# Moving the last layer's closing product of the last three images behind everything else, by channel chunk

## The chip, the core and the metric

The kernel runs on one core of a Trainium2 chip. A core has engines that run side by side, each in its own instruction order: TensorE (PE in the profile: matmuls; PEld: its weight loads), VectorE (DVE), ScalarE (ACT), GpSimd (POOL) and SyncE (SP), which here issues nearly all transfers; 16 DMA engines carry these between DRAM, where inputs and outputs live, and the on-chip memory (SBUF). Matmul results land in PSUM, a small memory of banks, and have to be evacuated by DVE or ACT. Engines wait for each other by semaphores. The metric is the device time of one execution in microseconds (us); a difference of about 0.2% can be told from none.

## What is computed

Two layers on eight images of 512 channels and 32 x 32 = 1024 positions, all in fp32. The first is an attention block, the second a non-local block with a batch normalization at its end. Cut to what matters:

```python
# layer 0
q, k, v = conv1x1(x, Wq, bq), conv1x1(x, Wk, bk), conv1x1(x, Wv, bv)   # 8 heads of 64
attn = softmax(einsum('bhdn,bhdm->bhnm', q, k) * 64 ** -0.5)
x = x + conv1x1(einsum('bhnm,bhdm->bhdn', attn, v), Wp, bp)
# layer 1
g, theta, phi = conv1x1(x, g_w, g_b), conv1x1(x, theta_w, theta_b), conv1x1(x, phi_w, phi_b)
f = einsum('bcn,bdn->bcd', theta, phi) / 1024          # 256 x 256 per image
z = conv1x1(einsum('bcd,bdn->bcn', f, g), W_w, W_b) + x
mean, var = z.mean(axis=(0, 2, 3)), z.var(axis=(0, 2, 3))
out = (z - mean) * rsqrt(var + 1e-5) * gamma + beta
```

The mean and the variance of a channel are over all eight images. No output value is known before the z of the last image is, and all 16.78 MB of output (eight images of four chunks of 128 channels, 512 KB each) are written after it.

## The kernel before, in words

The program is one stream written out for the images 0 to 7. A planner places the instructions of each engine, with semaphores for what depends on what; matmuls are kept in the order in which they are written (`pe`). On-chip memory is handed out by pools: a pool with n buffers makes the allocation number n + 1 wait until the first is free. The ones that matter here:

- `ring` (11 blocks of 512 KB, `block`): the exponentials `e`, and after the attention the sums `t_o`, `t_x`, the weight `ww` and the product `wf`.
- `w3` (tag `acc`, 3): the running sums `acc` of the exponentials, and later in the image the two halves of `g`.
- `wr` (tag `w`, 2): the weights in use, which are fetched from DRAM again for every image (`load_w`).
- `xp` (2): the x of the image at work and of the next one. `mats` has one buffer each for `v`, `q`, `k` and `o`; the tile `tp` takes the place of `o`.
- `psS`: three PSUM tiles of two banks, taken in turn (`next_bank`), for scores and large products; `psO`: two more.

For every image: attention (scores, L300; exp on ACT, L303; weighted sums, L332 to L335), with the q and v products of the next image drawn in near its end; the k product of the next image; `project` (L399), which adds the projection to x in place; `theta_phi`; then `nonlocal_` (L424): g (`pg`), f (`pf`, L434), wf = f times W (`pwf`, L452), and z = wf times g + x (`pz`).

Large products are made by `seven` (L169): seven products of half-size blocks in the place of eight, the blocks being sums that DVE makes beforehand (`data_sums`, L151; for the z product L466 and L469). Each product is evacuated or added up by DVE or ACT.

For images 0 to 6 the z product is one of these (L486): 14 matmuls, evacuated into x, whose statistics (`bn_stats`, L489) follow. z of images 0 to 5 is then written to DRAM (`spill`, L491); z of image 6 stays in its buffer (`KEEP = 2`). For image 7 `last_z` makes the plain product, 16 matmuls, chunk by chunk; as soon as a chunk has its statistics, `batch_norm` (L508) turns mean and variance into scale and shift, applies them to the eight tiles of that chunk, DVE and ACT taking turns, and writes each tile out (L523). Before this, from the end of image 7's attention on, z of images 0 to 5 is fetched back: three into `v`, `q` and `k`, one into `fold`, image 5 into four ring blocks (L537), image 3 into the place of `o`, once `pf` has used up `tp`.

All those transfers are on SP's queue, and SP issues them in the planned order: one that waits holds up those behind it.

A matmul in fp32 makes two entries in the trace, so the profile's counts of matmuls are twice those of the program.

Of the kernel before, what the change touches and what calls it, by code (L numbers as in the profile page):

```python
# [8 lines left out]
F32 = mybir.dt.float32  # L9
I32 = mybir.dt.int32  # L10
AF = mybir.ActivationFunctionType
# [5 lines left out]
P = 128  # L17
# [13 lines left out]
def unshifted(ctx: ExitStack, tc: tile.TileContext, a: dict, out: bass.AP):  # L31
# [8 lines left out]
    NPAIR = HEADS // 2  # L40
    CI = a["WgT"].shape[1]
    IC = CI // P
    KEEP = 2
    RUN = 6
    LEAD = 128

# [17 lines left out]
    def pe(ins):  # L64
        tc.keep_in_program_order(ins)
# [6 lines left out]
    def next_bank(name):  # L72
        free.append(free.pop(0))
        return bank(free[-1], name)

    def block(name):
        return ring.tile([P, 2, 512], F32, tag="e", name=name)
# [153 lines left out]
        nc.vector.memset(heads[j * D:(j + 1) * D, j * D:(j + 1) * D], 1.0)  # L231
    mv = const.tile([P, CC, 2], F32, tag="mv", name="mv")
    gates = const.tile([P, B * NPAIR], F32, tag="gates", name="gates")
    spill = [dram.tile([P, CC, N], F32, tag=f"spill{b}", name=f"spill{b}") for b in range(B - KEEP)]

    def halves(t):
        return t.rearrange("p (h n) -> p h n", h=NH)
# [183 lines left out]
              lambda q, ps: nc.vector.tensor_tensor(at(q), at(q), as_tp(ps), ALU.add))  # L421
        return tp

    def nonlocal_(b, xt, data, tp, wg, before_z):  # L424
        ww = block(f"ww_{b}")
        nc.sync.dma_start(ww, a["WwT"].rearrange("(c p) f -> p c f", p=P))
        g = [w3.tile([P, N], F32, tag="acc", name=f"g_{b}_{d}") for d in range(IC)]
        f = w2.tile([P, IC, CI], F32, tag="ri", name=f"f_{b}")

        def make_f():  # L430
            ps = psO.tile([P, 512], F32, tag="o", name=f"pf_{b}").rearrange("p (c d) -> p c d", c=IC)
            for c in range(IC):
                for i in range(NB):
                    pe(nc.tensor.matmul(ps[:, c, :], tp[:, i, c * P:(c + 1) * P], tp[:, i, CI:],  # L434
                                        start=(i == 0), stop=(i == NB - 1)))
            nc.scalar.mul(f, ps, 1.0 / N)

        def part(q):
            return g[int(q[0]) - 1][:, cols(q)]

        def first(q, ps):
            d = int(q[0]) - 1
            nc.scalar.activation(part(q), ps[:, 0, :], AF.Identity, bias=gb[:, d:d + 1])  # L443

        seven(f"pg_{b}", wg, data, False, first,
              lambda q, ps: nc.vector.tensor_tensor(part(q), part(q), ps[:, 0, :], ALU.add), {5: make_f})

        wf = block(f"wf_{b}")
        for d in range(IC):
            ps = psO.tile([P, 512], F32, tag="o", name=f"pwf_{b}_{d}")  # L450
            for c in range(IC):
                pe(nc.tensor.matmul(ps, f[:, c, d * P:(d + 1) * P], ww[:, c, :], start=(c == 0), stop=(c == IC - 1)))  # L452
            nc.scalar.copy(wf[:, d, :], ps)
        if before_z:
            before_z()
            last_z(b, xt, wf, g)
            return
        half = C // 2
        ws = block(f"ws_{b}")
        w = [wf[:, 0, :half], wf[:, 1, :half], wf[:, 1, half:]] + [ws[:, i, j * half:(j + 1) * half]  # L460
                                                                 for i in range(2) for j in range(2)]
        tg = block(f"tg0_{b}"), block(f"tg1_{b}")
        t = [tg[i // 2][:, i % 2, :] for i in range(4)]
        b11, b12, b21, b22 = (g[k][:, h * 512:(h + 1) * 512] for k in range(2) for h in range(NH))
        for to, l, r in ((t[0], b12, b11), (t[1], b22, t[0]), (t[2], b22, b12), (t[3], b21, t[1])):
            nc.vector.tensor_tensor(to, l, r, ALU.subtract)  # L466
        for to, l, r, op in ((3, wf[:, 0, half:], w[2], ALU.add), (4, w[3], w[0], ALU.subtract),
                             (5, w[0], wf[:, 0, half:], ALU.subtract), (6, w[1], w[4], ALU.subtract)):
            nc.vector.tensor_tensor(w[to], l, r, op)  # L469

        class Blocks:
            shape = (P, 7, 1, half)

            def __getitem__(self, at):
                _, i, k, m = at
                return w[i][:, m]

        def first_z(q, ps):
            for m in range(2):
                c = rows(q).start + m  # L480
                at = xt[:, c, cols(q)]
                nc.vector.scalar_tensor_tensor(at, ps[:, m, :], wb[:, c:c + 1], at, ALU.add, ALU.add)  # L482

        data = {"11": b11, "21": b21, "22": b22, "t1": t[0], "t2": t[1], "t3": t[2], "t4": t[3]}
        data = {n: d.rearrange("p (k n) -> p k n", k=1) for n, d in data.items()}
        seven(f"pz_{b}", Blocks(), data, False, first_z, add_to(xt))  # L486
        for oc in range(CC):
            for h in range(NH):
                nc.vector.bn_stats(stats[:, oc, b * NH + h, :], xt[:, oc, h * 512:(h + 1) * 512])  # L489
            if b < B - KEEP:  # L490
                nc.sync.dma_start(spill[b][:, oc, :], xt[:, oc, :])  # L491

    def last_z(b, xt, wf, g):

        z[b] = [xt[:, oc, :] for oc in range(CC)]
        for oc in range(CC):
            for h in range(NH):
                ps = next_bank(f"pz_{b}_{oc}_{h}")[:, 0, :]
                s = slice(h * 512, (h + 1) * 512)
                for d in range(IC):  # L500
                    pe(nc.tensor.matmul(ps, wf[:, d, oc * P:(oc + 1) * P], g[d][:, s],
                                        start=(d == 0), stop=(d == IC - 1)))
                nc.vector.scalar_tensor_tensor(xt[:, oc, s], ps, wb[:, oc:oc + 1], xt[:, oc, s],
                                               ALU.add, ALU.add)
                nc.vector.bn_stats(stats[:, oc, b * NH + h, :], xt[:, oc, s])
            batch_norm(oc)

    def batch_norm(oc):  # L508

        nc.vector.bn_aggr(mv[:, oc, :], stats[:, oc, :, :].rearrange("p s k -> p (s k)"))  # L510
        gs, shift = (small.tile([P, 1], F32, tag=n, name=f"{n}_{oc}") for n in ("gs", "shift"))
        nc.scalar.activation(gs, mv[:, oc, 1:2], AF.Sqrt, bias=eps)
        nc.vector.reciprocal(gs, gs)
        nc.vector.tensor_tensor(gs, gs, gamma[:, oc:oc + 1], ALU.mult)
        nc.vector.tensor_tensor(shift, mv[:, oc, 0:1], gs, ALU.mult)
        nc.vector.tensor_tensor(shift, beta[:, oc:oc + 1], shift, ALU.subtract)
        for i, b in enumerate(sorted(z, reverse=True)):
            t = z[b][oc]
            if i % 2:
                nc.scalar.activation(t, t, AF.Identity, bias=shift, scale=gs)  # L520
            else:
                nc.vector.tensor_scalar(t, t, gs, shift, ALU.mult, ALU.add)
            nc.sync.dma_start(out_v[b, :, oc, :], t)  # L523

    z = {}

    def reload(b, tag):
        t = mats.tile([P, CC, N], F32, tag=tag, name=f"z_{b}")
        for cc in range(CC):
            nc.sync.dma_start(t[:, cc, :], spill[b][:, cc, :])  # L530
        z[b] = [t[:, cc, :] for cc in range(CC)]
# [5 lines left out]
            nc.sync.dma_start(t, spill[b][:, cc, :])  # L537
            z[b].append(t)

    def reload_fold(b):  # L540
        t = foldp.tile([P, CC, N], F32, tag="fold", name=f"z_{b}")
        for cc in range(CC):
            nc.sync.dma_start(t[:, cc, :], spill[b][:, cc, :])
        z[b] = [t[:, cc, :] for cc in range(CC)]


    data = data_sums(quarters_of(xt), "x_0")
    q, peak_q = heads_of(0, "q", weights("WqT"), bq, data, order=(0, 5, 1, 2, 3, 4, 6))
    load_w(nc.sync)
    bv, bp, gb, wb, gamma, beta = (load_col(n, nc.sync) for n in ("bvc", "bp", "gb", "Wb", "gamma", "beta"))  # L550
    tpb = const.tile([P, 2, 1, CI], F32, tag="tpb", name="tpb")
    nc.sync.dma_start(tpb[:, 0, 0, :], a["theta_b"].partition_broadcast(P))
    nc.sync.dma_start(tpb[:, 1, 0, :], a["phi_b"].partition_broadcast(P))
# [4 lines left out]
    for b in range(B):  # L558
# [19 lines left out]
        if not last:  # L578
            v = nxt["v"]
            k, peak_k = heads_of(b + 1, "k", weights("WkT"), bk, nxt["data"])  # L580
            load_w(nc.sync)
            q, peak_q = nxt["q"], nxt["peak_q"]
            between = {4: lambda: bound_scores(b + 1, q, k, peak_q, peak_k)}
        else:
            for i, tag in enumerate("vqk"):
                reload(i, tag)
            reload_fold(4)
            reload_chunks(5)
        w = weights("WpT")
        if b == 0:  # L590
            join_bias(w)
        project(b, xt, o, w, between)
        load_w(nc.sync)
        data = data_sums(quarters_of(xt), f"x1_{b}")
        tp = theta_phi(b, weights("tp"), data)
        load_w(nc.sync)
        nonlocal_(b, xt, data, tp, weights("WgT"), (lambda: reload(3, "o")) if last else None)
        load_w(nc.sync)
        if B - KEEP <= b < B - 1:
            z[b] = [xt[:, cc, :] for cc in range(CC)]  # L600
        xt = nxt.get("x")


    good = const.tile([P, 1], F32, tag="good", name="good")
# [216 lines left out]
```

## Time and profile before

The time before is 2242.79 us, the median of three runs (2241.12 to 2243.93). The profiled execution has a span of 2242.5 us.

| what | before |
|---|---|
| PE busy, entries | 2187.0 us (98%), 8306 |
| DVE busy, instructions | 1306.7 us (58%), 1273 |
| ACT busy, instructions | 692.8 us (31%), 814 |
| DMA, moved in all | 202.26 MB, mean 90 GB/s |
| mean clock granted to PE | 0.989 |
| z of image 7 begins | 2186.3 us |
| first output issued | 2196.9 us |
| last output issued in the stretch that begins | 2228.1 us |

The views used below are: the page, with the busy time of each engine and the chain of work that ended last, followed back from the last instruction; the same chain in order of time, one line for each piece (start, length, engine, tile and line); the timeline (all instructions in order of time, merged where alike); and stretches, the busy time of each engine between two times, with the clock granted to PE, the share of the DMA engines that is busy and what they moved. The groups list instructions by line, engine, operation and tile with the count, then the busy time in us and the mean of one in ns, then the idle time before them. Names of tiles stand as output<-inputs.

### The profile page before, as it was taken

The page shows a single profiled execution, that of the slowest core. Times are in us where ns is not written, and L with a number is a line of the kernel's source. Part 1 is how long each engine was busy: PE and PEld are TensorE (multiplying, and loading weights), DVE is VectorE, ACT ScalarE, POOL GpSimd, SP SyncE. Part 2 cuts the span into 40 slices and gives each one's busy share as a digit, 9 for nine tenths or more (in the row PEclk, how much of TensorE's full clock was granted, in tenths as well). Part 3 has the DMA queues.
Part 4 walks back from the last instruction along what each step waited for, and adds up shares of the span by engine and source line. Part 5 has one row for each costly group of instructions (what it writes and reads, how often), then busy time and mean ns, then how long its engine had stood idle before and what let it go on. Part 6 is the DMA issues. An engine that isn't in the chain of part 4 may idle for free.

```text
span 2242.5 us, 21033 instructions
## 1 busy us (share of the span) xinstructions
PE 2187.0 (98%) x8306; PEld 1108.8 (49%) x8306; DVE 1306.7 (58%) x1273; ACT 692.8 (31%) x814; POOL 35.4 (2%) x36
## 2 busy tenths in 40 slices
PE   8999999999999999999999999999999999999992
PEld 3634664346633556335563365533664346643361
DVE  4476446763477644775447744577356664467734
ACT  1453104531045210552106510254103531035303
POOL 0000000000000000000000000000000000000000
PEclk9999999999999999999999999999999999999996
DMA  6212223122131222322223221322214122210517
GB/s 234 85 29 89 92 99 127 36 78 89 59 133 46 77 73 91 104 62 66 83 79 108 58 88 64 120 59 62 90 59 150 29 61 90 91 52 20 211 51 313
DMA packets 57081, 202.26 MB, mean 90 GB/s; under 512 B 10256, under 2 KB 16656, under 8 KB 51856
## 3 DMA queue, kind: packets, MB, share of 16 engines
q1 hardware_dynamic: 55600, 199.80, 26.8%
q8 instruction: 67, 1.10, 0.2%
q10 hardware_dynamic: 1376, 1.05, 0.1%
q14 instruction: 38, 0.31, 0.0%
HBM read 125.98 MB, written 43.38 MB: 76 GB/s over the span
## 4 chain that ended last, share of the span: by engine, by line
PE 96%; DVE 2%; DMA 0%; ACT 0%; issue 0%; ACTq 0%; DVEq 0%
PE ps L300 20%; PE po L335 18%; PE pv L189 9%; PE pp L189 9%; PE ptp L189 9%; PE pk L189 9%; PE pq L189 8%; PE pg L189 4%; PE pz L189 3%; PE pf L434 2%; PE po L333 1%; PE pwf L452 1%; PE po L332 1%; PE den L335 1%; DVE x L482 0%; DMA a_WqT<-in_WqT_dram 0%
## 5 line engine op out<-in xcount | busy, mean ns | idle before, releaser
L303 ACT ACTIVATE e<-ps 128x1024 f32<-128x1024 f32 x512 | 485.8, 1040 | 353.0 <-PE ps L300 311.3
L309 DVE TENSOR_TENSOR acc<-acc,e 128x1024 f32<-128x1024 f32 x384 | 470.3, 1225 | 156.0 <-ACT e L303 123.7
L300 PE MATMUL ps<-q,k 64*128 64x512 f32 x2048 | 462.7, 599 | 0.0
L335 PE MATMUL po<-e,v 128*64 128x512 f32 x1872 | 458.5, 595 | 0.0
L300 PEld LDWEIGHTS ps<-q,k 64*128 64x128 f32 x2048 | 187.5, 186 | 273.0 <-issue 162.9
L335 PEld LDWEIGHTS po<-e,v 128*64 128x64 f32 x1872 | 148.0, 137 | 214.9 <-issue 205.8
L443 ACT ACTIVATE g<-pg,gb 128x512 f32<-128x512 f32 x32 | 22.0, 687 | 430.0 <-PE pg L189 430.0
L189 PE MATMUL pp<-t_o,w_WpT 128*128 128x512 f32 x256 | 115.6, 600 | 3.1 <-DVE t_o L155 3.1
L189 PE MATMUL pq<-t_x,w_WqT 128*128 128x512 f32 x256 | 114.0, 593 | 2.0 <-DVE q L206 1.5
L189 PE MATMUL pv<-w_WvT,t_x 128*128 128x256 f32 x512 | 114.5, 379 | 0.0
L189 PE MATMUL ptp<-w_tp,t_x 128*128 128x256 f32 x512 | 114.4, 379 | 0.0
L189 PE MATMUL pk<-t_x,w_WkT 128*128 128x512 f32 x256 | 113.8, 592 | 0.0
L206 DVE TENSOR_TENSOR k<-k,pk 128x1024 f32<-128x1024 f32 x24 | 29.3, 1221 | 142.5 <-PE pk L189 142.5
L189 PEld LDWEIGHTS ptp<-w_tp,t_x 128*128 128x128 f32 x512 | 97.3, 190 | 13.2
L189 PEld LDWEIGHTS pv<-w_WvT,t_x 128*128 128x128 f32 x512 | 97.1, 190 | 13.2
L307 DVE TENSOR_TENSOR acc<-e,e 128x1024 f32<-128x1024 f32 x64 | 77.7, 1213 | 36.9 <-ACT e L303 36.4
L248 ACT ACTIVATE q<-pq,bq 128x512 f32<-128x512 f32 x64 | 40.5, 683 | 180.7 <-PE pq L189 180.6
L189 PE MATMUL pq<-x,w_WqT 128*128 128x512 f32 x192 | 89.8, 613 | 5.7 <-DMA w_WqT<-in_WqT_dram 5.7
L189 PE MATMUL pp<-o,w_WpT 128*128 128x512 f32 x192 | 89.5, 610 | 0.0
L248 ACT ACTIVATE k<-pk,bk 128x512 f32<-128x512 f32 x64 | 40.4, 683 | 153.6 <-PE pk L189 153.6
L189 PE MATMUL pv<-w_WvT,x 128*128 128x256 f32 x384 | 87.5, 381 | 0.0
L189 PE MATMUL ptp<-w_tp,x 128*128 128x256 f32 x384 | 86.8, 379 | 0.0
(126 smaller groups left out, 2018.3 us busy)
## 6 DMA issues: line engine op xcount, KB each, us to landing
fold<-acc SPq DMA_DIRECT2D x240, 128.0 KB, 2.3
x<-in_x_dram SPq DMA_DIRECT2D x32, 512.0 KB, 5.9
r<-den_d SPq DMA_DIRECT2D x120, 128.0 KB, 3.0
w_WqT<-kept_WqT SPq DMA_DIRECT2D x7, 1792.0 KB, 7.3
w_WvT<-kept_WvT SPq DMA_DIRECT2D x7, 1792.0 KB, 7.2
w_WkT<-kept_WkT SPq DMA_DIRECT2D x7, 1792.0 KB, 7.1
w_WpT<-kept_WpT SPq DMA_DIRECT2D x7, 1792.0 KB, 7.0
w_tp<-kept_tp SPq DMA_DIRECT2D x7, 1792.0 KB, 7.2
```

Of the source, the lines that this page charges most:

```text
L189: pe(nc.tensor.matmul(to_ps, lhsT(k), rhs(k), start=(s, at) not in begun, stop=(k == nk - 1), skip_group_check=True))
L206: nc.vector.tensor_tensor(at, at, ps, ALU.add)
L248: nc.scalar.activation(t[:, c, cols(q)], ps[:, m, :], AF.Identity, bias=bias[:, c:c + 1])
L300: pe(nc.tensor.matmul(ps[:, j, :], k[r, p, m * P:(m + 1) * P], q[r, p, h * 512:(h + 1) * 512], start=True, stop=True))
L303: nc.scalar.activation(e, ps, AF.Exp, scale=SCALE)
L307: nc.vector.tensor_tensor(accs[u], es[u, 0], e, ALU.add)
L309: nc.vector.tensor_tensor(accs[u], accs[u], e, ALU.add)
L332: pe(nc.tensor.matmul(to[:, :LEAD], l, r[:, :LEAD], start=start, stop=False, skip_group_check=True))
L333: pe(nc.tensor.matmul(to[:, LEAD:], l, r[:, LEAD:], start=False, stop=stop, skip_group_check=True))
L335: pe(nc.tensor.matmul(to, l, r, start=start, stop=stop, skip_group_check=True))
L434: pe(nc.tensor.matmul(ps[:, c, :], tp[:, i, c * P:(c + 1) * P], tp[:, i, CI:], start=(i == 0), stop=(i == NB - 1)))
L452: pe(nc.tensor.matmul(ps, f[:, c, d * P:(d + 1) * P], ww[:, c, :], start=(c == 0), stop=(c == IC - 1)))
```

## The change

The z product of images 5, 6 and 7 (`LATE = 3`) is no longer made with the image, but at the very end, for all three together, one chunk of 128 channels after the other. A chunk's statistics are complete once its three products are done, and its eight tiles can be written while PE makes the next chunk. For this the kernel has to keep what the product needs:

- x of image 5 is written to DRAM before the product instead of z after it, and comes back into four ring blocks (`reload_chunks`); images 6 and 7 keep their buffers.
- g and wf of images 5 and 6, 1.57 MB each, are written to DRAM (`put_away`) and come back into the two weight buffers when image 7 has no more use for them (`take_back`).
- The late products are plain: 16 matmuls each, where images 5 and 6 had 14 with the sums for them. A chunk of an image is evacuated in one instruction of 1024 columns.
- Which image is in which place changes: 0, 1 and 2 in `v`, `q`, `k`, image 3 in `fold`, image 4 in the place of `o`. Image 5's reload stands after the projection in the text, no longer before it.
- Scale and shift take one instruction less after the square root (`ngamma` is prepared at the start). They are written after the first evacuation of the next chunk, and DVE's order in this part is fixed (`dve`). ACT applies seven of the eight tiles of a chunk, four of the last one.

```diff
@@
-    KEEP = 2
+    LATE = 3
@@ def nonlocal_
+        before_wf()
         wf = block(f"wf_{b}")
...
-        if before_z:
-            before_z()
-            last_z(b, xt, wf, g)
+        if b >= B - LATE:
+            late[b] = xt, g, wf
             return
@@
+    def put_away(b):
+        xt, g, wf = late[b]
+        for d in range(IC):
+            nc.sync.dma_start(spill_g[b][:, d * N:(d + 1) * N], g[d])
+        nc.sync.dma_start(spill_g[b][:, IC * N:], wf)
+
+    def take_back(b):
+        t = wr.tile([P, IC * N + IC * C], F32, tag="w", name=f"gwf_{b}")
+        nc.sync.dma_start(t, spill_g[b])
...
+    def last_z():
+        order = [B - LATE, B - 1, *range(B - LATE + 1, B - 1)]
+        begun = None
+        for oc in range(CC):
+            for n, b in enumerate(order):
+                _, g, wf = late[b]
+                ps = next_bank(f"pz_{b}_{oc}")
+                for h in range(NH):
+                    for d in range(IC):
+                        pe(nc.tensor.matmul(ps[:, h, :], wf[:, d, oc * P:(oc + 1) * P], g[d][:, h * 512:(h + 1) * 512],
+                                            start=(d == 0), stop=(d == IC - 1)))
+                t = z[b][oc]
+                dve(nc.vector.scalar_tensor_tensor(t, ps.rearrange("p h n -> p (h n)"), wb[:, oc:oc + 1], t,
+                                                   ALU.add, ALU.add))
+                if n == 0 and begun:
+                    finish(oc - 1, *begun)
+                for h in range(NH):
+                    dve(nc.vector.bn_stats(stats[:, oc, b * NH + h, :], t[:, h * 512:(h + 1) * 512]))
+            begun = begin(oc)
+        finish(CC - 1, *begun)
...
+    def finish(oc, gs, shift):
+        dve(nc.vector.reciprocal(gs, gs))
+        dve(nc.vector.scalar_tensor_tensor(shift, shift, gs, beta[:, oc:oc + 1], ALU.mult, ALU.add))
+        dve(nc.vector.tensor_tensor(gs, gs, gamma[:, oc:oc + 1], ALU.mult))
+        for i, b in enumerate(sorted(z)):
+            t = z[b][oc]
+            if i == 0 or oc == CC - 1 and i % 2 == 0:
+                dve(nc.vector.tensor_scalar(t, t, gs, shift, ALU.mult, ALU.add))
+            else:
+                nc.scalar.activation(t, t, AF.Identity, bias=shift, scale=gs)
+            nc.sync.dma_start(out_v[b, :, oc, :], t)
@@ for b in range(B)
             for i, tag in enumerate("vqk"):
-                reload(i, tag)
-            reload_fold(4)
-            reload_chunks(5)
+                reload(i, mats, tag)
+            reload(3, foldp, "fold")
...
+        if b == B - LATE:
+            for cc in range(CC):
+                nc.sync.dma_start(spill[b][:, cc, :], xt[:, cc, :])
         data = data_sums(quarters_of(xt), f"x1_{b}")
+        if last:
+            reload_chunks(B - LATE)
+        elif b > B - LATE:
+            z[b] = [xt[:, cc, :] for cc in range(CC)]
...
+        def before_wf():
+            if last:
+                z[b] = [xt[:, cc, :] for cc in range(CC)]
+                take_back(B - LATE + 1)
+                reload(4, mats, "o")
+
+        if last:
+            take_back(B - LATE)
-        nonlocal_(b, xt, data, tp, weights("WgT"), (lambda: reload(3, "o")) if last else None)
+        nonlocal_(b, xt, data, tp, weights("WgT"), before_wf)
         load_w(nc.sync)
-        if B - KEEP <= b < B - 1:
-            z[b] = [xt[:, cc, :] for cc in range(CC)]
+        if b in spill_g:
+            put_away(b)
         xt = nxt.get("x")
+
+    last_z()
```

More of the change, by code (lines that the diff above doesn't have):

```diff
@@ L233, in unshifted @@
     gates = const.tile([P, B * NPAIR], F32, tag="gates", name="gates")
-    spill = [dram.tile([P, CC, N], F32, tag=f"spill{b}", name=f"spill{b}") for b in range(B - KEEP)]
+    ngamma = const.tile([P, CC], F32, tag="ngamma", name="ngamma")
+    spill = [dram.tile([P, CC, N], F32, tag=f"spill{b}", name=f"spill{b}") for b in range(B - LATE + 1)]
+    spill_g = {b: dram.tile([P, IC * N + IC * C], F32, tag=f"spillg{b}", name=f"spillg{b}")
+               for b in range(B - LATE, B - 1)}
     def halves(t):
@@ L422, in theta_phi, with nonlocal_ @@
         return tp
-    def nonlocal_(b, xt, data, tp, wg, before_z):
+    def nonlocal_(b, xt, data, tp, wg, before_wf):
         ww = block(f"ww_{b}")
@@ L489, in nonlocal_ @@
                 nc.vector.bn_stats(stats[:, oc, b * NH + h, :], xt[:, oc, h * 512:(h + 1) * 512])
[L490 to L523, printed above, removed]
@@ L525, in unshifted @@
-    z = {}
-    def reload(b, tag):
-        t = mats.tile([P, CC, N], F32, tag=tag, name=f"z_{b}")
+            nc.sync.dma_start(spill[b][:, oc, :], xt[:, oc, :])
+    late, z = {}, {}
+    def put_away(b):
[6 more added lines that the diff above has]
+        nc.sync.dma_start(t, spill_g[b])
+        late[b] = (late[b][0], [t[:, d * N:(d + 1) * N] for d in range(IC)],
+                   t[:, IC * N:].rearrange("p (d c) -> p d c", d=IC))
@@ L529, in reload @@
+    def reload(b, pool, tag):
+        t = pool.tile([P, CC, N], F32, tag=tag, name=f"z_{b}")
         for cc in range(CC):
@@ L538, in reload_chunks, with dve @@
             z[b].append(t)
[L540 to L544, printed above, removed]
+    def dve(ins):
+        tc.keep_in_program_order(ins)
+    def last_z():
[18 more added lines that the diff above has]
+        finish(CC - 1, *begun)
@@ new lines, in begin @@
+    def begin(oc):
+        dve(nc.vector.bn_aggr(mv[:, oc, :], stats[:, oc, :, :].rearrange("p s k -> p (s k)")))
+        std, shift = (small.tile([P, 1], F32, tag=n, name=f"{n}_{oc}") for n in ("gs", "shift"))
+        nc.scalar.activation(std, mv[:, oc, 1:2], AF.Sqrt, bias=eps)
+        dve(nc.vector.tensor_tensor(shift, mv[:, oc, 0:1], ngamma[:, oc:oc + 1], ALU.mult))
+        return std, shift
+    def finish(oc, gs, shift):
[9 more added lines that the diff above has]
+            nc.sync.dma_start(out_v[b, :, oc, :], t)
@@ L550, in unshifted @@
     bv, bp, gb, wb, gamma, beta = (load_col(n, nc.sync) for n in ("bvc", "bp", "gb", "Wb", "gamma", "beta"))
+    nc.vector.tensor_scalar(ngamma, gamma, -1.0, 1.0, ALU.mult, ALU.mult)
     tpb = const.tile([P, 2, 1, CI], F32, tag="tpb", name="tpb")
```

## The prediction, made before the changed kernel was run

> **What bounds the kernel now.** I read the page first (busy time, then the chain that ended last), then that chain in order of time around the places the change touches, then the stretches of the tail.
>
> ```profile
> PE 2187.0 (98%) x8306; PEld 1108.8 (49%) x8306; DVE 1306.7 (58%) x1273; ACT 692.8 (31%) x814; POOL 35.4 (2%) x36
> PE 96%; DVE 2%; DMA 0%; ACT 0%; issue 0%; ACTq 0%; DVEq 0%
> ```
>
> TensorE (PE) is the path nearly everywhere: a matmul taken out of the middle is time saved, one for one, unless another wait follows. The z of image 6 on the chain (image 5's lies the same, at 1706.55):
>
> ```profile
> 1977.96 1.73 PE pz L189 x4
> 1981.51 8.90 PE pz L189 x20
> 1990.42 10.70 PE ps L300 x48
> ```
>
> From its first product to the first scores of the next image it takes 1990.42 - 1977.96 = 12.46 us, all of it PE's. The third place is the projection of image 7, after attention:
>
> ```profile
> 2114.71 1.32 DVE x L404 x2
> 2116.03 1.14 DVE t_o L155
> 2117.21 22.56 PE pp L189 x48
> ```
> ```profile
> 1907.17:1931.43 24.26, 24.26 (x60) 10.87 (x59) 12.98 (x17) 1.26 (x2) 4.40 (x4) 1.00 0.22 76
> 2110.45:2139.60 29.15, 26.08 (x58) 11.25 (x57) 18.41 (x17) 0.00 (x0) 0.00 (x0) 0.94 0.46 170
> 2117.20:2121.20 4.00, 3.99 (x6) 1.69 (x7) 3.49 (x3) 0.00 (x0) 0.00 (x0) 0.57 1.02 409
> ```
>
> VectorE (DVE) evacuates x before it makes t_o, and PE stands idle 3.07 us for that t_o. The stretches (columns: length, busy PE, PEld, DVE, ACT, POOL, PE clock, DMA share, GB/s) show the projection of image 6, 24.26 us, and of image 7, 29.15 us: 4.9 us more, since after the idle time the clock was 0.57 for 4 us.
>
> Then the tail. The z of image 7 begins at 2186.31 (call this T) and the first output is issued at 2196.88, T + 10.6:
>
> ```profile
> 2186.31 3.53 PE pz L501 x8
> 2196.88 0.81 SPq L523 DMA_DIRECT2D out_dram<-x  x2
> 2197.00:2203.00 6.00, 3.33 (x10) 1.29 (x8) 6.00 (x13) 5.08 (x5) 0.00 (x0) 0.98 0.90 356
> 2208.00:2214.00 6.00, 0.00 (x0) 0.00 (x0) 5.86 (x12) 6.00 (x7) 0.00 (x0) 0.50 1.03 401
> 2232.00:2238.00 6.00, 0.00 (x0) 0.00 (x0) 0.00 (x0) 0.00 (x0) 0.00 (x0) 0.50 1.02 409
> ```
>
> From 2197 to 2239 the DMA engines are full at 400 to 409 GB/s while PE does almost nothing: 32 tiles of 512 KB, 16.78 MB, which cannot leave before the batch statistics are complete. The chain view ends at ACT and shows no DMA here; the stretches do. The span ends at 2242.5, 45.6 us after the first issue. So the end is set by T, by how soon after T the first output goes, and by 45.6 us of output; PE time moved behind T is free as long as output stays fed.
>
> **What the Trainium skill says.** "DMA: Bandwidth & Descriptors", Specifications, gives a fabric ceiling of 435 GB/s; the trace reaches 409, so output cannot go much quicker. "TensorE: Matmul & The Clock Gate", What's actually happening: PE's clock falls to half after an idle window of about 3.4 us and returns after about as long busy. The trace agrees: 3.07 us idle, then 0.57; but 1.8 us of waiting at 2071 left it at 1.00. "VectorE: DVE Perf Modes", Mode 2x_2P: two results a cycle for fp32 with one tensor source in SBUF, not for a PSUM operand. The trace agrees (rows below): a 1024-wide tensor_scalar takes 0.81 us, the 512-wide evacuation of PSUM already 0.74.
>
> ```profile
> L520 ACT ACTIVATE z<-z,shift,gs 128x1024 f32<-128x1024 f32 x12 | 14.0, 1226 | 0.0
> L522 DVE TENSOR_SCALAR z<-z,gs,shift 128x1024 f32<-128x1024 f32 x12 | 9.0, 808 | 0.0
> L503 DVE SCALAR_TENSOR_TENSOR x<-pz,Wb,x 128x512 f32<-128x512 f32 x8 | 5.9, 737 | 13.4 <-PE pz L501 13.4
> L505 DVE BATCH_NORM_STATS2 stats<-x 128x6 f32<-128x512 f32 x8 | 5.5, 682 | 0.1
> ```
>
> **1. z of images 5 and 6 leaves the middle.** 2 x 12.46 = 24.9 us less PE before T. In the built program scores follow pwf directly; the DVE sums for the seven products, 16 evacuations and statistics go too, so DVE comes earlier to the next attention. Gain 24.9.
>
> **2. The projection of image 7.** The reload of image 5 into the ring now comes after t_o's blocks, and in the built order the first t_o stands ahead of the last acc: ready long before PE wants it. But the next three t_o now stand between the two evacuations of x, and the third product writes the bank which the second of these empties. DVE is done with o at 2114.7; x 0.7, three t_o of 1.13 (their spacing in the trace), x 0.7: 2119.5. PE, without the old wait, is through two products of 3.43 at 2110.45 + 6.9 = 2117.3. It idles 2.2 instead of 3.07 us. Bounds: 0.9 gained if the clock still falls, 4.9 - 2.2 = 2.7 if not (1.8 us did not do it). I take 2.7.
>
> **3. Put away and take back.** g and wf of images 5 and 6, 1.57 MB each, go to DRAM and return. They hold two acc buffers and one ring block. In the ring of 11, the wf block is wanted again by the eleventh exp of the next attention, 3.4 (pwf) + 10 x 0.93 + 0.9, some 13.6 us after the end of pg. Queued on SP behind a 1.79 MB weight load (7.3 us to landing on the page) come two pieces of 0.52 MB, at 344 GB/s (2.1 MB in 6.1 us of DMA time at 2181) 1.5 us each: landed at about 10.5. Behind them the queue holds the first fold, not wanted sooner. Cost 0, bound 0 to 2 us per image. For the return, image 5's load waits for tp's slot, free at the end of ptp, 22 us ahead of use. Image 6's waits for WgT's slot, free at the end of pg, T - 3.4. Ahead of it in the queue is half of z_4 (1 MB, issued at T - 5.1). Landing T - 3.4 + 7.3 + 1.5 = T + 5.4; first use, third in the order, T + 6.9. Cost 0, bound 0 to 3; the first outputs of chunk 0 stand behind it.
>
> **4. The tail.** PE has 48 matmuls of two passes for 16: 0.43 us a pass (13.98 us for 32), so 3.44 us per image and chunk, 10.3 per chunk. A 1024-wide evacuation is not in the trace: 1.2 us by the nearest row (adding z from PSUM, 1.205), 1.49 if it were two of 512. I take 1.2. First output: T + 10.3 (third image), evacuation 1.2, two statistics 1.3, aggregate 0.6, shift 0.1, then by the written order the next chunk's first evacuation, for which PE is ready at T + 13.8: T + 15.0; three small ones 0.45, tensor_scalar 0.8, issue: T + 16.5, 5.9 later than now. After that, per chunk: PE 10.3; DVE 3 x 1.2 + 6 x 0.68 + 0.6 + 0.1 + 0.45 + 0.8 = 9.6; ACT 7 x 1.16 (spaced 3.49 for three) + 0.3 = 8.4; output 42/4 = 10.5. Output is the slowest, by little. Sum: T + 16.5 + 45.6 = T + 62.1, against T + 56.2.
>
> **Sum.** T moves by -24.9 - 2.7 to 2158.7; the end is 2220.8, 21.7 earlier: 2242.8 - 21.7 = **2221 us**.
>
> **Rivals.** *Forecast*, 0.74: for it, full DMA with an idle PE over 36 us. *New waits*, 0.13: the wf block 2 + 2, the late take-back 3, the clock in step 2 1.8, a DMA gap of 1 us at each chunk since output leads PE by only 0.2: 2233. For it, the slacks of 1.5 to 3 us; against, each must fail. *DVE bounds the tail*, 0.08: 1.49 per evacuation and waits of 0.1 to 0.2 at each of its 17 instructions make 12.5 per chunk; last chunk at T + 16.5 + 37.5, plus 0.7 + 10.5 + 3.1: 2227. For it, 9.6 against 10.3; against, the spacing in the trace is under the single durations. *Slower*, 0.05: PE waits on PSUM each chunk and the clock stays at 0.50, as it stood in the tail: 20.6 per chunk, T + 26.8 + 61.8 + 14.3 = T + 103: 2262. Against, the 0.50 stands where PE had no instructions, and three banks let it run ahead.
>
> **How the numbers follow.** The range takes the whole project gain (2219) and an output start 3 to 5 us sooner than my chain of small operations as low end, 2214, and the new waits as high end, 2233. Faster by over 0.2% in the first three cases, 0.95; within 0.01; slower 0.04.
>
> **What would show it.** Step 1: scores right after pwf for images 6 and 7. Step 2: the pp wait about 2 us and clock near 1. Step 3: no PE wait on gwf or ACT on wf's landing. Step 4: pz beginning near 2159, first output 16 to 17 us later, DMA at 400 GB/s from there to the end. A gap in DMA at a chunk border, or a wait of fold on a put-away, would make it wrong.

## The result, and the profile after

| | before | changed |
|---|---|---|
| time, median of 6 runs each | 2242.02 us (2240.18 to 2243.93) | 2223.3 us (2221.6 to 2226.62) |
| ratio, 95% interval | | 0.9918 (0.9905 to 0.9931) |
| span of the profiled execution | 2242.5 us | 2221.3 us |
| begin of the late z (T) | 2186.31 us | 2158.23 us |
| first output issued | T + 10.57 | T + 16.45 |
| end | T + 56.2 | T + 63.1 |

The change saves 18.7 us of the medians. The forecast was 2221 us.

The changed kernel's page, with the busy times and the shares of the chain that ended last:

```profile
PE 2187.9 (98%) x8314; PEld 1111.1 (50%) x8314; DVE 1285.3 (58%) x1231; ACT 703.3 (32%) x823; POOL 35.4 (2%) x36
PE 97%; DVE 1%; DMA 0%; ACT 0%; issue 0%; DVEq 0%
```

PE is busy for 0.9 us more than before, in a span 21 us shorter. The totals tell nothing of the gain: the work was moved, not cut. The chain in order of time (start, length, piece) tells it:

```profile
1960.07 3.43 PE pwf L456 x8
1963.50 10.70 PE ps L303 x48
...
2092.57 19.13 PE pp L189 x40
2111.70 24.17 PE ptp L189 x112
...
2154.80 3.43 PE pwf L456 x8
2158.23 41.21 PE pz L536 x96
```

The scores `ps` of image 7 follow `pwf` of image 6 without a gap (1960.07 + 3.43 = 1963.50), where 12.46 us of `pz` stood. All of the z product left is one piece of 41.21 us at the end. Cut at matching places, the two profiled executions differ like this:

| piece | before | after | difference |
|---|---|---|---|
| start to the first `ptp` of image 0 | 303.00 | 300.99 | -2.0 |
| z of image 5, z of image 6 | 12.46 + 12.46 | none | -24.9 |
| attention of image 7, first scores to projection | 120.11 | 120.11 | 0 |
| projection of image 7 to `ptp` | 29.25 | 28.09 | -1.2 |
| `ptp` to T | 46.53 | 46.53 | 0 |
| T to the first output | 10.57 | 16.45 | +5.9 |
| first output to the end | 45.6 | 46.6 | +1.0 |

The sum is -21.2 us. The first row does not come from the change (last section); without it the profiles differ by 19.2 us, close to the 18.7 of the medians.

The tail in the timeline of the changed kernel (start, length, instruction, count, and in brackets the idle time before it with what ended it). some of DVE's instructions first, then the first of SP's issues for each chunk:

```profile
2168.57 1.28 DVE L539 SCALAR_TENSOR_TENSOR x<-pz,Wb,x 128x1024 f32<-128x1024 f32 x1 [0.83 <-PE pz L536]
...
2171.21 0.59 DVE L549 BATCH_NORM_AGGREGATE mv<-stats 128x2 f32<-128x96 f32 x1
...
2172.01 1.28 DVE L539 SCALAR_TENSOR_TENSOR z<-pz,Wb,z 128x1024 f32<-128x1024 f32 x1
...
2173.84 0.81 DVE L563 TENSOR_SCALAR z<-z,gs,shift 128x1024 f32<-128x1024 f32 x1
...
2174.68 5.45 SPq L566 DMA_DIRECT2D out_dram<-z  x6
...
2184.99 5.46 SPq L566 DMA_DIRECT2D out_dram<-z  x6
...
2195.28 5.49 SPq L566 DMA_DIRECT2D out_dram<-z  x6
...
2204.55 6.95 SPq L566 DMA_DIRECT2D out_dram<-z  x6
```

The chunk's third image is evacuated at 2168.57, its statistics are complete at 2171.8, but the next chunk's evacuation (2172.01, 1.28 us) goes ahead of the scale; the first tile leaves at 2174.68. The chunks follow each other at 10.3 us, the pace of PE; the last comes after 9.3 us, since no evacuation of a next chunk stands ahead of its scale. The stretches (length, busy PE, PEld, DVE, ACT, POOL, PE clock, DMA share, GB/s) show what this buys:

```profile
2176.00:2182.00 6.00, 6.00 (x15) 2.66 (x14) 5.38 (x7) 5.92 (x6) 0.00 (x0) 1.00 1.02 406
2187.00:2192.00 5.00, 5.00 (x13) 2.13 (x13) 4.38 (x7) 5.00 (x5) 0.00 (x0) 1.00 1.02 404
2208.00:2214.00 6.00, 0.00 (x0) 0.00 (x0) 0.00 (x0) 0.34 (x1) 0.00 (x0) 0.50 1.02 398
```

The DMA engines are as full as in the tail before, and now PE works at full clock beside them. What was idle time of PE during the output now holds the products.

### The profile page after: what moved, and what is told of

It is laid out like the page before. It is cut to its first block, busy times and chain, and to the rows that moved or that the text cites. A ratio compares the mean times of both kernels' runs of the same rounds, so it can differ in the third digit from the quotient of the medians.

```text
span 2221.3 us, 21043 instructions
## 1 busy us (share of the span) xinstructions
PE 2187.9 (98%) x8314; PEld 1111.1 (50%) x8314; DVE 1285.3 (58%) x1231; ACT 703.3 (32%) x823; POOL 35.4 (2%) x36
## 3 DMA queue, kind: packets, MB, share of 16 engines
HBM read 129.12 MB, written 46.53 MB: 79 GB/s over the span
## 4 chain that ended last, share of the span: by engine, by line
PE 97%; DVE 1%; DMA 0%; ACT 0%; issue 0%; DVEq 0%
PE ps L303 21%; PE po L338 18%; PE pv L189 9%; PE pq L189 9%; PE ptp L189 9%; PE pk L189 9%; PE pp L189 9%; PE pg L189 4%; PE pf L437 2%; PE pz L189 2%; PE pz L536 2%; PE po L336 1%; PE pwf L456 1%; PE po L335 1%; PE den L338 1%; DVE x L485 0%
## 5 line engine op out<-in xcount | busy, mean ns | idle before, releaser
L189 PEld LDWEIGHTS ptp<-w_tp,t_x 128*128 128x128 f32 x512 | 97.4, 190 | 13.1
```

Of the source, the lines that this page charges most:

```text
L189: pe(nc.tensor.matmul(to_ps, lhsT(k), rhs(k), start=(s, at) not in begun, stop=(k == nk - 1), skip_group_check=True))
```

## The experiments

The theory: time falls by the PE time taken out of the middle (12.46 us an image) because the tail is bound by output and hides the products; the price is the later first output. Rivals: the gain comes from the other edits (the mended projection, the rewritten tail); or the tail is free whatever stands in it. Every kernel but half_before starts from the changed one, and distances from T are used throughout, since T carries the chance variation of everything ahead of it.

### How many images are late: late1, late2, late4

```diff
-    LATE = 3
+    LATE = (7,)            # (6, 7);  (4, 5, 6, 7)
...
-        if b >= B - LATE:
+        if b in LATE:
             late[b] = xt, g, wf
...
-        order = [B - LATE, B - 1, *range(B - LATE + 1, B - 1)]
+        order = [7]            # [6, 7];  [5, 7, 6, 4]
```

The cut shows late1; the comments give the values of late2 and late4. The edits that serve no late image stay as they are: the shorter chain after the square root, the 1024-wide evacuations, the fixed order on DVE and the reload of image 5 behind the projection. An image that is not late is made with its image as before, and nothing of it is put away. In late4 the g and wf of image 4 come back into three ring blocks.

> Only image 7's product at the end; images 5 and 6 made with their images as before, all other edits of the change kept (the shorter chain after the square root, 1024-wide evacuations, DVE order, reload after the projection). Theory (the gain is PE time moved behind the output): projection -1.0, first output at T + 9.7 in place of 10.6: -0.9, so 2240 us beside 2242 of before. Rival (the gain comes from the other edits): 2223 to 2226.

> Images 6 and 7 at the end, image 5 as before. Theory: one z less on PE before T, -12.5; projection -1.0; first output at T + 13.1, +2.5: 2231 us. Between one, two and three late images the steps are then equal, -9.0 each (12.46 gained, 3.44 of later first output lost). Rival (put away and take back cost something fixed, which a second image does not pay again): the first step is the smaller one, 2233 or more.

> Images 4 to 7 at the end (g and wf of image 4 come back into three ring blocks). Theory: 12.46 more leave the middle, but a chunk is now 13.75 of PE against 10.5 of output, so the tail is PE's: first output T + 19.9, last chunk's first tile T + 60.3, end near T + 75; 2222 us, no more than 1 or 2 from three late images. DMA engines idle some 3 us before each later chunk. Rival (output remains the bound): another -9.0, 2214.

| | T | first output | end | median | ratio to before |
|---|---|---|---|---|---|
| late1 | 2180.75 | T + 9.7 | T + 55.6 | 2241.23 | 0.9993 (0.9985 to 1.0001) |
| late2 | 2167.78 | T + 13.0 | T + 58.7 | 2231.68 | 0.9951 (0.9938 to 0.9965) |
| changed (3) | 2158.23 | T + 16.45 | T + 63.1 | 2223.3 | 0.9918 (0.9905 to 0.9931) |
| late4 | 2145.15 | T + 21.5 | T + 76.2 | 2224.2 | 0.9917 (0.9904 to 0.9931) |

With image 7 alone late, all the other edits together are worth 1.6 us; the interval reaches from a loss of 0.2 to 3.4 us, far from 18.7: the first rival falls. The second late image brings 9.5 us of median, the third 8.4 (7.5 where each is set against the runs of the kernel before that were taken with it), each near 12.46 less the 3.3 to 3.4 us by which the first output moves. The fourth brings nothing. Late4's output issues, and PE's longest wait in its tail, in two views:

```profile
2166.65 5.47 SPq L573 DMA_DIRECT2D out_dram<-z  x6
...
2180.38 5.44 SPq L573 DMA_DIRECT2D out_dram<-z  x6
...
2194.11 5.45 SPq L573 DMA_DIRECT2D out_dram<-z  x6
...
2206.82 5.49 SPq L573 DMA_DIRECT2D out_dram<-z  x6
```
```profile
PE pz L543 <- DVE x L546: 1.4, 1, 1.4
```

The first three chunks come 13.7 us apart, four products of 3.43 us, while the output of a chunk takes about 10.3 us. So the DMA engines run dry at each border; in the stretches of late4:

```profile
2172.00:2176.00 4.00, 4.00 (x11) 1.82 (x10) 3.10 (x5) 1.89 (x2) 0.00 (x0) 1.00 1.03 408
2176.00:2180.00 4.00, 4.00 (x10) 1.71 (x9) 3.81 (x9) 0.76 (x2) 0.00 (x0) 1.00 0.47 183
```

The 13.1 us by which T moved are given back in the tail (76.2 - 63.1 = 13.1). Three is where PE's pace per chunk, 10.3, just matches that of the output. The second rival falls too. The first output came 1.6 us later than expected, most of it the 1.4 us that PE waited once for DVE to empty a PSUM bank.

### Half the output: half_before, half_after

```diff
-            nc.sync.dma_start(out_v[b, :, oc, :], t)
+            if b % 2 == 0:
+                nc.sync.dma_start(out_v[b, :, oc, :], t)
```

The same edit is made in the kernel before and in the changed one. Both leave out the writing of the images 1, 3, 5 and 7; all values are still computed.

> The kernel before, with only the even images written out (the output of images 1, 3, 5 and 7 is left out, every tile is still computed). Theory: the end is set by 42 us of output; half of it goes, 21 us, and the tail then ends about where ACT is done with the last tile: 2222 us.

> The changed kernel with the same half of the output left out. Theory: with 5.2 us of output per chunk the 10.3 us of PE per chunk are no longer hidden; the last chunk's first tile goes out at T + 46.3 as before, 5.2 of output, 4 to the end: 2215 us, so that 7 of the 19 us of gain are left. Rival (late products are cheaper as such, hidden or not): 2203, the gain stays at 19.

Half_before took 2224.6 us (0.9917, 0.9900 to 0.9933, of the full kernel before), half_after 2215.3 us (0.9882, 0.9866 to 0.9899). With half the output the change is worth 9.3 us, not 18.7; an estimate from the two intervals puts it between 3 and 13 us. The expectation was 7: half_after came as expected, and half_before took 2.6 us longer than the 2222 expected of it. The gain is halved although T came 28.9 us earlier (2183.79 and 2154.89): the tail grew by 18.0 us (from T + 38.4 to T + 56.4) in place of 6.9. In half_before the DMA engines are not full all through the tail either (274 GB/s from 2205 to 2210), so that its end is set in part by DVE and ACT. In half_after's stretches DMA is never full, and the products, no longer hidden, set the pace:

```profile
2176.00:2182.00 6.00, 6.00 (x15) 2.66 (x14) 5.78 (x11) 4.08 (x6) 0.00 (x0) 1.00 0.43 175
2187.00:2192.00 5.00, 5.00 (x13) 2.19 (x12) 4.78 (x11) 3.03 (x4) 0.00 (x0) 1.00 0.37 151
```

So about half of the gain goes when half of the output is taken away, as it must if the gain is PE's work hidden beside output. The rival that late products are cheaper as such, hidden or not, would have given 2203 us, and falls.

### The projection of image 7: order3

```diff
...
+            nc.vector.tensor_tensor(t[0], b12, b11, ALU.subtract)
...
+            def rest():
+                for to, l, r in ((t[1], b22, t[0]), (t[2], b22, b12), (t[3], b21, t[1])):
+                    mark(nc.vector.tensor_tensor(to, l, r, ALU.subtract))
+            between = {0: rest}
```

For the last image both evacuations of x now stand ahead of the last three `t_o` on DVE; `mark` is `dve`, which keeps the order.

> Three late images, and in the projection of image 7 both evacuations of x before the last three t_o on DVE. Theory: the wait of PE (1.9 us) and the slow clock after it (1.8 us) both go: 3.7 less than the changed kernel, 2219.6 us, the projection 24.3 long and PE's clock 1.00. Rival (DVE is late there anyway, the wait moves to a later product): 2222 to 2223.

It took 2219.72 us, 0.9900 (0.9885 to 0.9915). The stretch of the projection:

```profile
2083.60:2107.90 24.30, 24.30 (x62) 11.49 (x61) 17.32 (x19) 0.00 (x0) 0.00 (x0) 1.00 0.31 104
```

PE no longer waits, and the projection takes 24.3 us as for the images 1 to 6, at a clock of 1.00. The tail is as it was (first output T + 16.46). Against the profile of the changed kernel this piece is 3.8 us shorter. Of these, 1.7 are a slow clock that four other executions of the same code did not have (step 2 below); against those it is 2.1 us. The medians, with intervals of some 3.5 us each way, agree but don't establish it alone: they differ by 3.6 us.

### An earlier first output: soon3, split3, own3

All three keep the edit of order3. Soon3 computes a chunk's scale at once:

```diff
-                if n == 0 and begun:
-                    finish(oc - 1, *begun)
...
-            begun = begin(oc)
-        finish(CC - 1, *begun)
+            finish(oc, *begin(oc))
```

Split3 adds to it that the third image of a chunk is evacuated in two halves of its PSUM tile, so that the first may go while PE makes the second:

```diff
+                if b == order[-1]:
+                    for h in range(NH):
+                        at = t[:, h * 512:(h + 1) * 512]
+                        dve(nc.vector.scalar_tensor_tensor(at, ps[:, h, :], wb[:, oc:oc + 1], at, ALU.add, ALU.add))
+                        dve(nc.vector.bn_stats(stats[:, oc, b * NH + h, :], at))
+                    continue
```

Own3, made after split3 was seen, gives each half a tile of its own:

```diff
...
+                        s, ps = slice(h * 512, (h + 1) * 512), psO.tile([P, 512], F32, tag="o", name=f"pz_{b}_{oc}_{h}")
+                        for d in range(IC):
+                            pe(nc.tensor.matmul(ps, wf[:, d, oc * P:(oc + 1) * P], g[d][:, s],
+                                                start=(d == 0), stop=(d == IC - 1)))
...
```

> Three late images, the projection's order mended, and scale and shift finished at once, no longer after the next chunk's first evacuation. Theory: the first output goes at T + 15.3 in place of T + 16.5, and all later chunks likewise, so output stays fed: 1.2 less than with the projection mended alone, 2218.5 us. Rival (DVE, which now waits for the square root at every chunk, falls behind PE, and output starves at the chunk borders): 2219.7 or more.

> The same, and the third image of each chunk evacuated in two halves of 512 columns, each followed by its statistics, so that the first half is done while PE makes the second. Theory: the first output at T + 14.1, another 1.2 less: 2217.3 us. Rival: output starves, no gain over the one before.

> Three late images, projection mended, scale and shift at once, and the two halves of the third image in two PSUM tiles of their own, so that the evacuation of the first half waits for its own four passes alone. Theory (the halves of one tile before waited together): first output at T + 14.2, against T + 15.4 with scale and shift at once; end at T + 60.9; 2217 us. Rival (the second half is then late in its turn, or output starves at the chunk borders): end at T + 62 or more.

> The kernel with the projection mended and scale and shift at once, unchanged, on the same chip as the one with halves in tiles of their own. Theory: T + 15.4 and T + 62.1 again, 2218.5 us, 1.2 above the other; what lies ahead of T differs by 1 to 2 us between executions, in image 0, whatever the kernel.

| | first output | end | median | ratio to before |
|---|---|---|---|---|
| order3 | T + 16.46 | T + 63.2 | 2219.72 | 0.9900 (0.9885 to 0.9915) |
| soon3 | T + 15.42 | T + 62.1 | 2218.41 | 0.9894 (0.9878 to 0.9911) |
| soon3_again | T + 15.42 | T + 62.1 | 2219.58 | 0.9897 (0.9881 to 0.9914) |
| split3 | T + 15.67 | T + 62.3 | 2221.54 | 0.9905 (0.9888 to 0.9921) |
| own3 | T + 14.75 | T + 61.5 | 2219.34 | 0.9897 (0.9880 to 0.9913) |

Soon3 does what was expected: 1.0 us earlier, most of the 1.28 us of the evacuation that stood in between. Split3 missed, by 1.6 us at the first output. Its timeline, the third product and the two halves of its evacuation:

```profile
2162.81 7.03 PE L549 MATMUL pz<-gwf 128*128 128x512 f32 x16
2166.45 0.75 DVE L555 SCALAR_TENSOR_TENSOR x<-pz,Wb,x 128x512 f32<-128x512 f32 x1 [0.83 <-PE pz L549]
...
2167.84 0.73 DVE L555 SCALAR_TENSOR_TENSOR x<-pz,Wb,x 128x512 f32<-128x512 f32 x1
```

The line of PE merges two images, 3.43 us each; the second of them ends at T + 10.31 = 2166.42 on the chain. The first half begins only then, and the second half waits for nothing. So in this program DVE waits for the last matmul on the tile, whichever half it reads, and the cut only added an instruction. In own3, with the halves in two tiles, it no longer does:

```profile
2160.31 1.29 DVE L565 BATCH_NORM_STATS2 stats<-x 128x6 f32<-128x512 f32 x2
2161.52 0.73 DVE L553 SCALAR_TENSOR_TENSOR x<-pz,Wb,x 128x512 f32<-128x512 f32 x1
...
2162.89 0.73 DVE L553 SCALAR_TENSOR_TENSOR x<-pz,Wb,x 128x512 f32<-128x512 f32 x1
```

PE had the first half ready at about 2160.7 (T = 2152.09, two images of 3.44, half of the third) but DVE was still at the statistics of the image before, until 2161.52. So half of the 1.2 us that were hoped for came (0.67 us, from T + 15.42 to T + 14.75). The gain is in the distances from T; the medians of order3, soon3 and own3 can't be told apart. Any of the three, at 2218 to 2220 us, is faster than the kernel before (no interval reaches above 0.9915), and by its trace some 2 to 5 us better than the changed one (2.1 to 3.8 in the projection, 0 to 1.7 in the tail); the intervals of their times overlap with that of the changed kernel, and so the times alone don't rank them.

## Why the prediction was right, step by step

*Step 1, z of the images 5 and 6.* Right: 24.9 us predicted, 24.9 measured, with scores straight after `pwf`.

*Step 2, the projection.* The wait was right, 1.91 us where 2.2 was worked out. The term that hung on the clock was not the same in every execution. The product after that wait and the one behind it, in the changed kernel, and then in half_after, whose code is the same there:

```profile
2092.57 5.40 PE L189 MATMUL pp<-t_o,w_WpT 128*128 128x512 f32 x8 [1.91 <-DVE x L407]
2097.81 3.60 PE L189 MATMUL pp<-o,w_WpT 128*128 128x512 f32 x8
```
```profile
2090.92 3.70 PE L189 MATMUL pp<-t_o,w_WpT 128*128 128x512 f32 x8 [1.91 <-DVE x L407]
2094.46 3.60 PE L189 MATMUL pp<-o,w_WpT 128*128 128x512 f32 x8
```

Eight passes took 5.40 us after the wait in the one, 3.70 in the other. Late1, late2 and late4 show 3.70 as well. So the gain came in four executions of five, 2.85 us (29.25 us became 26.4) where 2.7 were taken, and in the one that was compared with before it was 1.2, near the lower bound. Finer stretches show the clock, first from the wait of the changed kernel on, then in the kernel before:

```profile
2090.66:2092.57 1.91, 0.00 (x1) 0.00 (x0) 1.91 (x4) 0.00 (x0) 0.00 (x0) 1.00 0.48 197
2092.57:2093.99 1.42, 1.42 (x4) 0.70 (x5) 1.26 (x2) 0.00 (x0) 0.00 (x0) 1.00 0.01 3
2093.99:2097.41 3.42, 3.42 (x6) 1.34 (x5) 0.00 (x0) 0.00 (x0) 0.00 (x0) 0.50 0.00 0
```
```profile
2117.38:2120.79 3.41, 3.41 (x5) 1.35 (x6) 3.31 (x3) 0.00 (x0) 0.00 (x0) 0.50 1.03 413
```

In both the clock stands at 0.50 for 3.4 us, which costs 1.7; the 0.57 over 4 us of the prediction is a mean over this stretch and a piece at 1.00. In the changed kernel the fall comes 1.4 us after PE is back at work. In the five executions without the wait (order3 and the kernels built on it) the clock stayed at 1.00 here. So the wait is a likely cause of the fall; why it came in only one of the five executions with the 1.91 us wait is open. Here the Trainium skill ("TensorE: Matmul & The Clock Gate", What's actually happening) names an idle window of about 3.4 us as what makes the clock fall; in these runs it fell after waits of 3.07 us and, once in five, of 1.91 us.

*Step 3, putting away and taking back.* Right at cost 0: attention of image 7 took 120.11 us in both kernels, no PE wait names `gwf`, and both pieces of the way back landed in time. The later one, image 6's, among the changed kernel's DMA issues from 2150 on (count, KB each, us to landing):

```profile
gwf<-spillg SPq DMA_DIRECT2D x1, 1536.0 KB, 8.4
```

It was issued at 2154.8 and so landed at 2163.2, T + 5.0 where T + 5.4 was worked out, 1.7 us ahead of its first use at 2164.9.

*Step 4, the tail.* The first output was predicted at T + 16.5 and came at T + 16.45; the evacuation of 1024 columns, taken at 1.2 us, measured 1.28; the chunks came every 10.3 us and DMA had no gaps. From the first issue to the end it took 46.6 us, not the 45.6 carried over from before; with one late image it took 45.9 and with two 45.7. The first 42.1 us of this and the rest, before and in the changed kernel:

```profile
2196.88:2238.98 42.10, 3.45 (x10) 1.33 (x8) 17.41 (x37) 17.55 (x17) 0.00 (x0) 0.57 1.00 397
2238.98:2242.49 3.51, 0.00 (x0) 0.00 (x0) 0.00 (x0) 0.00 (x0) 0.00 (x0) 0.50 0.11 43
```
```profile
2174.68:2216.78 42.10, 24.96 (x60) 10.85 (x58) 29.58 (x48) 28.83 (x28) 0.00 (x0) 0.84 1.00 395
2216.78:2221.33 4.55, 0.00 (x0) 0.00 (x0) 0.00 (x0) 0.00 (x0) 0.00 (x0) 0.50 0.13 51
```

The output went at nearly the same rate in both, 397 and 395 GB/s, worth 0.2 us over the whole. The rest of the microsecond lies behind the full stretch, where the last packets run out and the program ends; what makes this end longer is not shown. Of the rivals, DVE as the bound (12.5 us per chunk) did not appear, and the slow clock in the tail neither: it was 1.00 while PE had work.

*The sum.* T was predicted at 2158.7 and measured at 2158.23. That is closer than the steps deserve, by luck: image 0 came 2.0 us earlier for reasons outside of the change, and step 2 gave 1.5 less than was taken. By the medians the forecast of 2221 lies 2.3 us under 2223.3; the gain was 18.7 where 21.7 was forecast. The 1.0 us at the end and, in some executions, the clock of step 2 are the terms in which the rest can lie; the medians can't split them further.

## What to carry to other kernels

Where a stage is bound by transfers and an engine idles in it, look for work that can be moved in after the last point where it is needed, and move as much as the transfers hide per piece: here three products of 3.43 us against 10.3 us of output, and a fourth gave back all it brought. What such a move costs is seen mostly in one number, the delay of the first transfer (5.9 us here), so the work should be cut along the unit in which results become final (here the channel chunk), and the chain from its last product to its first transfer kept free of other instructions. When a gain is a few us, compare distances from an event just ahead of the change, not totals.

## What the runs showed of the hardware that was not expected

The clock granted to PE differs from one execution to the next at the same place. Besides the 1.91 us wait above, there is the small product with the bias `bp` in image 0 (32 matmul entries with one column each). Its stretch, before and in order3:

```profile
271.80:276.20 4.40, 4.40 (x34) 4.40 (x33) 2.85 (x6) 1.26 (x2) 0.00 (x0) 0.77 0.59 181
```
```profile
271.00:274.50 3.50, 3.50 (x34) 3.50 (x33) 2.15 (x5) 1.27 (x2) 0.00 (x0) 1.00 0.56 179
```

The same instructions took 4.4 us at a mean clock of 0.77 and 3.5 us at 1.00, and the eight passes after them 6.15 us before, where 3.60 is the usual. Cut finer, the stretch at half clock is 6.83 us long in the kernel before, 3.41 in the changed kernel, and missing in order3; the first two:

```profile
274.18:281.01 6.83, 6.83 (x16) 4.01 (x17) 3.95 (x8) 0.00 (x0) 0.00 (x0) 0.50 0.21 62
```
```profile
274.69:278.10 3.41, 3.41 (x7) 1.71 (x7) 3.01 (x7) 0.00 (x0) 0.00 (x0) 0.50 0.17 55
```

By the profile PE was not idle there; what makes the clock fall in some executions and not in others is not settled. But the fall orders what lies ahead. Over the twelve profiled executions of this case, the first `ptp` of image 0 starts at 298.7 to 299.6 us in the six without a fall (mean clock from 250 to 290 us 1.00), at 300.3 to 301.4 in the four with the short one (0.96), and at 302.7 to 303.0 in the two with the long one (0.91: before and split3). The change adds one small DVE instruction ahead of this place, and the experiments change nothing there. So the -2.0 us in the first row of the table above goes with a shorter fall. Single runs of one kernel differ by 2.5 us (split3) to 7.2 us (half_after), and this can be a good part of it: own3's four runs took 2215.43 us at a mean clock of 0.996, 2219.08 and 2219.61 at 0.995, and 2221.08 at 0.994.

The output kept 395 GB/s over 42.1 us while PE worked for 25 of them, DVE for 30 and ACT for 29, against 397 GB/s with PE nearly idle: moving the products under it slowed it by next to nothing.
